# Four recurrent, attention and expert layers in one kernel: the instruction order is laid down on another timing model

## The chip, the core and the metric

The kernel runs on one core of a Trainium2 chip, as one program. The core has five engines with a queue each: TensorE for matmuls (PE in the profile, with its weight loads as PEld), VectorE (DVE), ScalarE (ACT), GpSimd (POOL) and SyncE (SP), which here only issues DMAs. The program gives each engine its instructions in a fixed order. The metric is the device time of one execution in microseconds (us), as the median of several runs.

## The reference

The input x holds 4 sequences of 1024 tokens with 128 features. Four layers follow one another; each has the form

```python
xn = _layernorm(x, axis=-1)
s = _Ln_attn_ref(xn, ...)          # the mixer
g = _silu(_Ln_ffn_ref(xn, ...))    # the gate
x = x + s * g
```

- Layer 0: a state space mixer (projection, rotation of the queries, RMS norm, a causal convolution of four taps, a recurrence over chunks, a gated norm) beside a feed-forward network whose activations and weights are rounded blockwise to a 4-bit float grid.
- Layer 1: attention between the 16 heads of one token, with entmax (a sort of 16 values, running sums, a threshold) in place of softmax, beside a mixture of eight experts, two of them chosen per token.
- Layer 2: a delta-rule recurrence with 2 x 16 states for each of 16 heads over the whole sequence, with a convolution, gates and a group norm, beside a second mixture of eight experts with bfloat16 products.
- Layer 3: causal attention over 1024 tokens with 16 heads of 8 features, with relative positions (the products of q with an embedding, shifted by one place per row), beside a feed-forward network.

## The kernel before

All arithmetic is on tiles of 128 partitions. x stays in SBUF (x_all) through layers 0 to 2 and goes through DRAM (x3) to layer 3. `tile_kernel` calls the layers one after the other.

Three things fix the order of the work.

First, the Python program. Its parts are generators that yield between small steps, and `weave` (L78) runs several of them side by side in proportion to their numbers of steps. In layer 0 a unit is half a sequence, eight units in all; `layer0` weaves the recurrence of a unit (`mixer0`), its feed-forward network (`ffn0`) and the first part of the next unit's mixer. Layer 1 does the same with `heads1` and `moe1`, and weaves in the preparation of layer 2's weights. In layer 3 the order is written out by hand: for each of 4 sequences and 4 groups of four heads, the eight query tiles of 128 rows are taken in the order 7, 0, 6, 1, 5, 2, 4, 3 (ORDER3), 128 units in all, and the loop in `layer3` issues in turn one step of the score stream (`scores3`), transposes of weights (L1807), a piece of the product with the values (`weigh3`), and work for later units.

Second, the scheduler of the Tile library. The program runs inside `with tile.TileContext(nc) as tc`. When this block ends, the library goes through all recorded instructions with their dependencies and lays down the order on each engine: it simulates the program, and an engine that is free in the simulation gets, of the instructions that are ready then, the one that came first in the program. Buffers of the tile pools are given out in the same pass. The order found so is fixed in the program that runs on the chip. Without an argument the simulation is the library's default one.

Third, the pools. The number of buffers of a pool limits how far work can run ahead. In layer 3 PSUM holds one tile of scores (four banks, tag sc), three of tag tr and one of tag o.

The lines that the rest speaks of:

- `Kit.fp4` (L166 on) rounds to the 4-bit grid in steps that alternate between DVE and POOL; its last product (L181, POOL) makes hm, which PE transposes at L567.
- `mixer0`: POOL rotates the queries into rq (L391, L392), ACT sums squares (L398, L399), DVE scales to hq (L403), PE transposes hq (L125, in the helper `transpose_tiles`). L486 is the matmul pg of a chunk's recurrence.
- `heads1`: POOL multiplies weights with values (L790, prod), DVE reduces the product (L785). L748 and L766 are POOL steps of entmax, L752 a running sum and L768 a comparison on DVE that need them.
- Layer 2: PE makes pv (L1185), DVE takes it out into V (L1186); POOL multiplies (L1395), DVE reduces into A (L1398); PE spreads expert shares (L224), DVE multiplies with them into xin (L1080).
- Layer 3: ACT copies the relative products from PSUM to r (L2035), SP stores them to DRAM (flat, L2038 and L2039) and loads them back sheared as rel (L2054 to L2060), POOL masks rel (L2064). PE makes scores (L2097), DVE takes them out of PSUM, adds rel and keeps a running minimum (L2105, L2112), ACT takes the exponential (L2119), DVE transposes the result in blocks of 32 (L1807, wT), PE multiplies with the values (L2133).

A score tile is read by DVE four times, once per head, and PE can fill it again only after that:

```python
sc = ps.tile([P, 4, 512], F32, tag="sc", name="score")
for j in range(4):
    nc.tensor.matmul(
        sc[:, j, 0 : last - first], q[at(j), 1 + t * P : 1 + n], kk[at(j), first:last], start=True, stop=True
    )
yield "products"
```

The function that the diff touches follows.

## Time and profile before

| | |
|---|---|
| median of three runs | 3198.6 us (3194.61 to 3202.84) |
| profiled execution, its own time | 3201.78 us |
| span of its instructions | 3199.8 us |
| mean granted TensorE clock | 0.738 of full |
| DVE busy | 2297.5 us (72%), 5558 instructions |
| PE busy | 2085.2 us (65%), 17041 matmuls |
| ACT busy | 1511.3 us (47%), 3278 instructions |
| POOL busy | 1165.9 us (36%), 1094 instructions |
| DMA | 333.13 MB, nearly all through one queue on SP |

How to read the lines that come later: a group or wait names the engine, what the instruction writes and the line of the kernel; "A <- B: total, times, longest" says that engine A stood idle in front of an instruction until B had ended, for so many microseconds in total. "issue" as a releaser means that the profile shows nothing that was waited for. A line of the timeline gives start, duration, engine, line, operation and operands, and in brackets the idle time of the engine in front of it with its releaser. In a table of stretches each row has its start and end, its length, the busy time of PE, PEld, DVE, ACT and POOL with their numbers of instructions, the granted clock of TensorE, the share of time in which the DMA engines moved data, and GB/s.

### The profile page before, as it was taken

How to read it: one execution, taken by the hardware profiler on the slowest of the kernel's cores; microseconds unless marked ns; L12 is line 12 of the kernel's file. 1: busy time of each engine (PE TensorE's matmuls, PEld its weight loads, DVE VectorE, ACT ScalarE, POOL GpSimd, SP SyncE). 2: the span in 40 equal slices, each digit the busy share in tenths (PEclk: the TensorE clock that was granted, in tenths of full speed). 3: DMA queues.
4: the chain of work that ended last, by engine and by line, in shares of the span. 5: the costliest groups of instructions: out<-in, count | busy, mean ns of one | idle time of the engine just before them, and what ended most of it. 6: DMA issues, size and time to landing. Idle time of an engine off the chain costs nothing. (4 is left out here: it accounts for less than half of the span.)

```text
span 3199.8 us, 47565 instructions
## 1 busy us (share of the span) xinstructions
PE 2085.2 (65%) x17041; PEld 1227.5 (38%) x17041; DVE 2297.5 (72%) x5558; ACT 1511.3 (47%) x3278; POOL 1165.9 (36%) x1094
## 2 busy tenths in 40 slices
PE   5787778577787766984443772455666666766754
PEld 2555556232233322661110232244444534544543
DVE  5555545878888886657777888567778787787777
ACT  3554544333333333435332562136766765764663
POOL 3334443134444444224468233232323322323322
PEclk9888888588878878995655575566766766766766
DMA  3000000100000000330343456248688677678772
GB/s 80 14 1 1 1 1 1 35 0 0 0 0 7 7 0 14 112 102 11 73 108 110 134 114 139 92 154 268 210 249 248 199 232 239 200 235 250 218 238 68
DMA packets 334064, 333.13 MB, mean 104 GB/s; under 512 B 25968, under 2 KB 307436, under 8 KB 328196
## 3 DMA queue, kind: packets, MB, share of 16 engines
q1 hardware_dynamic: 332676, 325.90, 34.4%
q10 hardware_dynamic: 1152, 4.19, 0.4%
q8 instruction: 134, 2.20, 0.3%
q14 instruction: 102, 0.84, 0.1%
HBM read 175.31 MB, written 154.14 MB: 103 GB/s over the span
## 5 line engine op out<-in xcount | busy, mean ns | idle before, releaser
L2119 ACT ACTIVATE neg<-neg,low 128x640 f32<-128x640 f32 (+7 forms) x512 | 390.1, 764 | 146.5 <-DVE low L2112 146.1
L1807 DVE STREAM_TRANSPOSE wT<-neg 128x640 f32<-128x640 f32 (+7 forms) x512 | 377.2, 761 | 18.0 <-ACT neg L2119 13.7
L2064 POOL TENSOR_SCALAR_AFFINE_SELECT rel<-rel 128x512 f32<-128x512 f32 x288 | 179.2, 635 | 549.5 <-DMA rel<-flat 388.2
L2112 DVE CUSTOM_DVE_ANT_0 neg<-score,rel,low 128x128 f32<-128x128 f32 (+3 forms) x448 | 211.8, 504 | 158.1 <-PE score L2097 62.8
L2133 PE MATMUL po<-wT,vb 128*32 128x64 f32 (+1 forms) x10240 | 258.5, 256 | 100.1 <-DVE wT L1807 52.2
L2133 PEld LDWEIGHTS po<-wT,vb 128*32 128x32 f32 x10240 | 211.4, 137 | 163.0 <-DVE wT L1807 76.9
L2097 PE MATMUL score<-k,q 32*128 32x512 f32 (+3 forms) x768 | 123.7, 557 | 180.6 <-DVE low L2112 180.0
L2035 ACT COPY r<-pr 128x512 f32<-128x512 f32 x256 | 135.2, 582 | 170.0 <-PE pr L2033 112.9
L2033 PE MATMUL pr<-emb,q 32*128 32x256 f32 x512 | 130.3, 445 | 70.8 <-ACT r L2035 52.6
L2112 DVE CUSTOM_DVE_ANT_0 neg<-score,rel 128x512 f32<-128x512 f32 (+3 forms) x320 | 149.6, 520 | 23.7 <-issue 9.6
L837 PE MATMUL pg<-xnT,w 128*128 128x512 f32 x256 | 149.3, 667 | 7.0 <-DVE h L841 3.9
L790 POOL TENSOR_TENSOR prod<-rest,kv 128x2048 f32<-128x2048 f32 x32 | 145.1, 4570 | 18.4 <-ACT rest L780 18.4
L840 ACT ACTIVATE h<-pg 128x512 f32<-128x512 f32 x128 | 75.9, 595 | 157.8 <-PE pg L837 154.4
L839 PE MATMUL pu<-xin,w 128*128 128x512 f32 x256 | 140.6, 632 | 12.9 <-DVE h L841 7.4
L828 PE MATMUL po<-h,w 128*128 128x512 f32 x256 | 129.7, 628 | 26.3 <-DVE h L841 26.3
L2097 PEld LDWEIGHTS score<-k,q 32*128 32x128 f32 x768 | 54.2, 232 | 223.8 <-DVE low L2112 177.8
L216 PE MATMUL pt<-ident,three 128*24 128x128 bf16 x64 | 9.2, 295 | 196.7 <-DVE three L213 196.7
L2033 PEld LDWEIGHTS pr<-emb,q 32*128 32x128 f32 x512 | 92.7, 270 | 111.9 <-ACT r L2035 72.6
L433 PE MATMUL px<-hT,xbcT 128*128 128x512 f32 x256 | 114.7, 592 | 0.0
L1086 PE MATMUL ph<-xin,upT 128*128 128x512 bf16 (+1 forms) x128 | 69.7, 575 | 65.7 <-DVE xin L1080 64.4
L1491 PE MATMUL read<-kt,const_sb 128*128 128x128 f32 x256 | 50.9, 371 | 90.3 <-POOL kt L1486 90.3
L785 DVE TENSOR_REDUCE s<-prod 128x128 f32<-128x2048 f32 x32 | 73.1, 2284 | 49.2 <-POOL prod L790 49.2
(633 smaller groups left out, 5749.5 us busy)
## 6 DMA issues: line engine op xcount, KB each, us to landing
flat<-r SPq DMA_DIRECT2D x128, 512.0 KB, 6.3
rel<-flat SPq DMA_DIRECT2D x112, 512.0 KB, 4.3
flat<-r SPq DMA_DIRECT2D x128, 256.0 KB, 6.3
rel<-flat SPq DMA_DIRECT2D x96, 256.0 KB, 4.7
kt<-kd SPq DMA_DIRECT2D x16, 512.0 KB, 4.6
qt<-qd SPq DMA_DIRECT2D x16, 512.0 KB, 5.7
kdc<-kdd SPq DMA_DIRECT2D x16, 512.0 KB, 8.6
ktc<-ktd SPq DMA_DIRECT2D x16, 512.0 KB, 6.2
```

The costliest lines, as they stand in the source:

```text
L790: nc.gpsimd.tensor_tensor(prod, attn.rearrange("p (t h g) -> p t h g", t=4, g=16)[:, t].unsqueeze(2).to_broadcast(each), kv[:, t, 1, :].re ...
L828: nc.tensor.matmul(po, W["w2"][:, e, c, :], h[:, c, :], start=(e == 0 and c == 0), stop=(e == 7 and c == 1))
L837: nc.tensor.matmul(pg, W["w1"][:, e, c * P : (c + 1) * P], xnT, start=True, stop=True)
L839: nc.tensor.matmul(pu, W["w3"][:, e, c * P : (c + 1) * P], xin, start=True, stop=True)
L1807: nc.vector.transpose(weights[at, pair][j][:, t % 2, 0 : (t + 1) * P], S[j][:, 0 : (t + 1) * P])
L2033: nc.tensor.matmul(to[:, m, :], q[at, t * P : (t + 1) * P], W["emb"][at, i, :], start=True, stop=True)
L2035: nc.scalar.copy(r[:, n], to)
L2064: nc.gpsimd.affine_select(out=rel[:, :, slot(back), :], in_=rel[:, :, slot(0), :], compare_op=op, fill=fill, base=0, pattern=[[0, 4], [-si ...
L2097: nc.tensor.matmul(sc[:, j, 0 : last - first], q[at(j), 1 + t * P : 1 + n], kk[at(j), first:last], start=True, stop=True)
L2112: nc.vector.tensor_tensor_reduce(out=neg[:, begin:last], in0=sc[:, j, begin - first : last - first], in1=rel[:, j, slot : slot + (last - b ...
L2119: nc.scalar.activation(neg[:, 0:n], neg[:, 0:n], AF.Exp, bias=here, scale=-1.0, accum_out=group["sums"][:, j, t : t + 1])
L2133: nc.tensor.matmul(o[32 * j : 32 * j + 32, 2 * pair + m.start : 2 * pair + 2, :], vb[:, kb % 4 * NT + kb // 4, j].rearrange("p a d -> p (a ...
```

## The change

The context is made with one more argument. With it the library's scheduler simulates on its timeline model in place of its default simulation, when it lays down the order of the instructions on each engine. The Python program, the tiles, the pools and the arithmetic are the same.

```diff
-    with tile.TileContext(nc) as tc:
+    with tile.TileContext(nc, schedule_with_timeline_sim=True) as tc:
         tile_kernel(tc, I, out)
```

## The prediction

> **What bounds the kernel now.** The change touches no instruction, only the order in which each engine gets its instructions. So I first read which engine limits each stage and how long it stands idle there; then who is waited for on that engine; then a few stretches of the timeline, to see whether such a wait is one that another order could fill. First, busy time by stretch (the stretches are cut at round times; layer 0 runs in the second one, layer 1 in the third, most of layer 2 in the fourth, the end of layer 2 and layer 3 in the fifth, where the first score matmul stands at 2152.8 us):
>
> ```profile
> core 0: us, PE busy (x) PEld busy (x) DVE busy (x) ACT busy (x) POOL busy (x), PEclk, DMA share, GB/s
> ...
> 60.00:560.00 500.00, 386.15 (x1858) 275.58 (x1856) 258.83 (x696) 256.33 (x590) 197.07 (x253) 0.87 0.02 7
> 560.00:1250.00 690.00, 501.99 (x1154) 206.57 (x1154) 556.87 (x787) 244.58 (x459) 264.41 (x116) 0.80 0.02 7
> 1250.00:1950.00 700.00, 422.24 (x1501) 198.76 (x1500) 514.94 (x1029) 297.78 (x587) 307.29 (x223) 0.69 0.34 95
> 1950.00:3150.00 1200.00, 728.06 (x11816) 516.94 (x11820) 905.04 (x2815) 683.15 (x1570) 368.90 (x457) 0.67 0.69 211
> ```
>
> PE limits layer 0 (386 of 500 us, 114 idle), DVE everything behind it (557 of 690, 515 of 700, 905 of 1200: 133, 185 and 295 idle). No stage has an engine that is always busy: 727 us of the 3090 are idle time of the limiting engine. That, and no more, is what an order can win; the busy sums stay. Second, who was waited for by that engine (us in total, times, longest), in layer 0, layer 1, layer 2 and layer 3:
>
> ```profile
> PE pt L125 <- DVE hq L403: 43.5, 7, 7.6
> PE pt L567 <- POOL hm L181: 42.2, 8, 5.7
> ```
> ```profile
> DVE s L785 <- POOL prod L790: 41.8, 24, 3.6
> DVE cum L768 <- POOL zz L766: 27.4, 8, 3.9
> DVE cum L752 <- POOL z L748: 11.9, 7, 2.1
> ```
> ```profile
> DVE V L1186 <- PE pv L1185: 44.3, 31, 6.7
> DVE A L1398 <- POOL gram L1395: 25.0, 17, 5.2
> DVE xin L1080 <- PE pb L224: 17.3, 25, 2.1
> ```
> ```profile
> DVE neg L2112 <- PE score L2097: 62.1, 17, 10.7
> DVE neg L2112 <- issue: 60.0, 30, 9.5
> DVE neg L2112 <- POOL rel L2064: 44.7, 14, 12.9
> ```
>
> The reader is to see two kinds. In layers 0 to 2 the waits are regular: seven or eight in the eight units of layer 0, 24 among the 32 products of layer 1. An order laid down by a simulation that takes a POOL or DVE step for shorter than it is would leave just that: the consumer is put at the head of its engine's queue too early, and everything behind it stands too. Sum: 43.5 + 42.2 = 85.7; 41.8 + 27.4 + 11.9 = 81.1; 44.3 + 25.0 + 17.3 = 86.6; together 253 us. In layer 3 they are rare and long: 17 waits for 192 score tiles (768 score matmuls, four to a tile), so 175 tiles are hidden already.
>
> Third, the timeline: one hole on PE in layer 0, and in layer 3 two score tiles whose wait DVE has nothing to hide with.
>
> ```profile
> 341.79 1.03 PE L510 MATMUL pst<-xdd,btm 128*128 128x256 f32 x4
> 348.77 1.11 PE L125 MATMUL pt<-const_sb,hq 128*128 128x128 f32 x4 [5.95 <-DVE hq L403]
> ...
> 352.45 0.63 PE L486 MATMUL pg<-xc 128*128 128x128 f32 x2
> ```
> ```profile
> 2422.64 0.75 DVE L2112 CUSTOM_DVE_ANT_0 neg<-score,rel,low 128x512 f32<-128x512 f32 x1 [0.68 <-PE score L2097]
> ...
> 2427.10 0.29 DVE L2112 CUSTOM_DVE_ANT_0 neg<-score,rel 128x128 f32<-128x128 f32 x1 [0.54 <-PE score L2097]
> ```
>
> PE stands 5.95 us in front of the transposes of hq. The pg matmul of L486 behind it (0.63 us) reads xc, which is older, and needed only to be ahead of it; what lies between them in the queue hangs on hq or on xq. So a good order fills a part of such a hole, not all of it.
>
> **The change, step by step.**
> *Instructions.* None is added, removed or resized by the program; 5558 on DVE, 17041 matmuls and 906 DMAs on SP stay. What can differ in number are semaphore waits and table loads on ACT. The trace has 177 ACT_TABLE_LOADs (the groups by line added up) of 1283 ns, 227 us. Between no load less (the functions needed stay) and half as many again (+114 us) I take nothing: ACT is busy at most 683 of 1200 us in any stretch and limits none. Without that cover, in layer 3, the exps (L2119) would be late for the transposes (L1807), which wait 13.7 us for them today.
> *How far the order moves.* Numbering the instructions as the program issues them and comparing with the order on each engine, the present order is displaced by a mean of 2.3 places on PE in layer 0, 5.2 on DVE in layer 1, 7.6 on DVE in layer 2 and 1.5 on DVE in layer 3 (there without L2112, whose numbers are not comparable). The generators fix the order by and large, and the scheduler moves things locally. I expect the new order to differ by as little, so the effect to be small.
> *Waits in layers 0 to 2.* Another order can remove between none and all of the 253 us, and can add waits as well. The nearest row is the hole above: 0.63 of 5.95 us could be filled by the one matmul that I could name, about a tenth; a lookahead over the other unit's work should find as much again. I take a fifth, **-51 us**. Next late there is the chain itself: POOL, ACT and DVE for hq and hm, under 55% busy, whose order cannot shorten it.
> *Layer 3, score tiles.* PE can fill the one score tile only when DVE has read it (L2097 waits 171 us for L2112 in this stretch, 102 times); DVE hides that behind transposes (L1807, 0.27 to 1.25 us each). Where none stands there, the wait is 0.54 to 0.68 us (above), 0.61 at the mean. At 175 covered tiles that is between 0 and +107 us; a better order could at most take the 62 away. This order is the one most nearly as the program gives it, so a new one has more to spoil than to mend: I take one tile in seven, 25 x 0.61 = **+15 us**.
> *Layer 3, SP and POOL.* All DMAs of the layer go through one queue on SP, where loads of rel wait 202.8 us for DVE and stores of r 193.5 us for ACT; a load put in front of a store holds it up. POOL waits 388 us for rel, but DVE only 44.7 for POOL. Between -45 and, if one load in ten of 208 comes later by a store's landing time (6.3 us), +131 I take 0: POOL's idle time covers it today.
> *Start and tail.* 60 us ahead and 50 behind; the last store waits for a chain that no order shortens: 0.
>
> The sum is -51 + 15 = -36 us. The profiled execution took 3201.8 us (span 3199.8); the median of the three runs is 3198.6, 3.2 less. I take the difference off the median: **3163 us**.
>
> [...] The rows say that the granted clock is 0.87 of full in layer 0 and 0.67 in layer 3. [...] The rows alone show the clock, not what it does in another order, and I leave it out.
>
> **Rivals.**
> *(a) No difference.* The new order comes out nearly as the old one, or the option does not act, or what is won in one stage is lost in the next: 3189 to 3208 us. For it: the small displacements, and that the limiting waits end on chains. Against it: three stages whose waits repeat in every unit.
> *(b) Slower: layer 3 loses its cover.* One mechanism: DVE's transposes no longer stand between the last read of a score tile and the first of the next. Price 0.61 us a tile, +107 us for all 175, and with no gain elsewhere 3306 us. It decides against the forecast's 51 us from 84 tiles on. For it: one score tile, DVE 75% busy and limiting, and a cover made of single transposes which ACT's exps release. Against: most tiles have two transposes ready there.
> *(c) Much faster.* Half of the 253 us goes and layer 3 keeps its order: -127, 3072 us. For it: the regularity of the waits. Against: the hole above.
>
> **Chances.** Faster by over 0.3%, which is about what a measurement of this kernel can tell from no change: 0.46 (the forecast and its neighbours 0.37, (c) 0.09). Within 0.3%: 0.12. Slower: 0.42, most of it (b) in part; the signs are nearly even because the same freedom that can fill a hole can open one. The range takes in (c) and nearly all of (b): 3075 to 3295 us; some 0.05 lies below and 0.1 above. The forecast's own range, one part in ten to one in three of the 253 with layer 3 at 0 to +30, is 3114 to 3203.
>
> **What would show it.** Right: PE's waits in front of L125 and L567 in layer 0, and DVE's in front of L785, shrink by a fifth or more; layer 3 takes as long as before, with about 40 waits of DVE for score tiles. Wrong: busy sums or the clock of a stage change by over 3%; more table loads with ACT limiting; or DVE waiting for score or rel far more often than 17 and 14 times. The forecast fails if these waits are chains rather than bad order, and if the new order moves far more than a few places.

## The result, and the profile after

| | before | after |
|---|---|---|
| median | 3196.8 us of 4 runs (3194.6 to 3202.8) | 3237.9 us of 4 runs (3233.0 to 3247.6) |
| ratio | | 1.0129 (95% interval 1.0101 to 1.0158) |
| profiled execution, span | 3201.8 us, 3199.8 us | 3247.6 us, 3245.9 us |
| DVE busy | 2297.5 us | 2408.5 us |
| ACT busy, instructions | 1511.3 us, 3278 | 1537.3 us, 3297 |

The change makes the kernel 1.3% slower (41 us by the medians); 36 us less were forecast. DVE, PE and POOL have as many instructions as before, ACT has 19 more. First to be read is where each layer begins and ends (first and last instruction of its lines in the trace; layer 1 without the two memsets at its head, L626 and L627; for layer 3 the stream of score matmuls, L2097):

| us | before | after | difference |
|---|---|---|---|
| start until layer 0's first instruction | 42.4 | 64.1 | +21.7 |
| layer 0 | 529.1 | 533.2 | +4.1 |
| layer 1 | 693.3 | 698.2 | +4.9 |
| layer 2 | 868.7 | 837.7 | -31.0 |
| layer 3, score stream | 1015.0 | 1060.3 | +45.3 |
| between and behind them | 51.3 | 52.4 | +1.1 |

The sum is the 46.1 us between the spans; it is 5 us more than between the medians, since the profiled execution of after is the longest of its four. Four things have to be explained, not one, and they have both signs. The table of stretches of after, cut at the layers, and below it that of before, cut at the same places of the program:

```profile
core 0: us, PE busy (x) PEld busy (x) DVE busy (x) ACT busy (x) POOL busy (x), PEclk, DMA share, GB/s
64.00:597.00 533.00, 405.20 (x1906) 293.14 (x1906) 279.34 (x713) 261.89 (x612) 201.87 (x260) 0.84 0.02 6
607.00:1304.00 697.00, 529.01 (x1154) 211.02 (x1153) 645.20 (x744) 242.43 (x454) 285.12 (x115) 0.80 0.02 5
1306.00:2144.00 838.00, 503.92 (x1848) 259.67 (x1848) 634.14 (x1341) 340.96 (x678) 365.10 (x265) 0.66 0.38 105
2154.00:3214.00 1060.00, 657.11 (x11752) 465.13 (x11748) 799.19 (x2537) 672.92 (x1513) 306.83 (x412) 0.67 0.70 216
```
```profile
42.00:571.00 529.00, 400.62 (x1911) 286.37 (x1910) 280.52 (x784) 267.80 (x622) 205.49 (x266) 0.87 0.02 7
580.00:1273.00 693.00, 511.08 (x1155) 207.81 (x1155) 559.64 (x750) 242.89 (x454) 274.37 (x115) 0.80 0.02 5
1275.00:2144.00 869.00, 498.72 (x1848) 261.37 (x1848) 634.33 (x1333) 342.78 (x680) 352.04 (x265) 0.67 0.36 101
2153.00:3168.00 1015.00, 644.90 (x11752) 454.92 (x11752) 786.68 (x2537) 642.87 (x1493) 307.52 (x412) 0.68 0.74 226
```

The reader is to see the second row: in layer 1 the busy time of DVE rises from 560 to 645 us with the same work, while the layer keeps its length. In layer 2 DVE's busy time is the same and the layer is 31 us shorter. In layer 3 ACT is 30 us busier, and DVE too is busier by 12.5 of the 45 us (799.2 against 786.7); the other 32.5 are idle time of DVE. The clock differs by 0.03 at most.

**Layer 1: waits became longer instructions.** The waits of after that answer to those of before, PE's in layer 0 (first two lines), then DVE's in layer 1 and in layer 2:

```profile
PE pt L125 <- DVE hq L403: 45.9, 8, 7.7
PE pt L567 <- POOL hm L181: 38.1, 9, 5.7
```
```profile
DVE s L785 <- POOL prod L790: 7.7, 5, 2.2
DVE cum L752 <- POOL z L748: 0.9, 1, 0.9
```
```profile
DVE V L1186 <- PE pv L1185: 31.0, 22, 5.8
```

In layer 0, cut at the layer, before had 50.1 and 48.2 us in the first two; in layer 2 it had 44.3. In layer 1, cut at the layer, it had

```profile
DVE s L785 <- POOL prod L790: 49.2, 28, 3.6
```

and 11.9 us at L752 and 27.4 at L768, which no longer stands in the list: 88.5 us have become 8.6. The forecast for that was a fifth; nine tenths went, and the layer gained nothing. Where they went is seen in the timeline, POOL's line first, then DVE's in the same time:

```profile
1139.81 9.31 POOL L790 TENSOR_TENSOR prod<-rest,kv 128x2048 f32<-128x2048 f32 x2 [3.04 <-ACT rest L780]
```
```profile
1139.30 0.66 DVE L698 TENSOR_TENSOR sorted<-sorted 128x384 f32<-128x384 f32 x1
1139.86 4.93 DVE L699 TENSOR_TENSOR sorted<-sorted 128x384 f32<-128x384 f32 x1
1144.70 0.68 DVE L841 TENSOR_TENSOR h<-h,pu 128x512 f32<-128x512 f32 x1
1145.30 4.38 DVE L698 TENSOR_TENSOR sorted<-sorted 128x512 f32<-128x512 f32 x1
```

A step of the sort (L698, L699: both operands in SBUF) takes 0.66 us just before POOL's product begins and 4.93 us beside it, about as long as one product (two in 9.31 us, so 4.65 at the mean); L841, one of whose operands lies in PSUM, takes 0.68 us in the same time (all 128 of it in after take 0.65 to 0.69 us; the 25 that lie wholly beside a POOL instruction 0.68 at the mean, the 71 beside none as well). In after, 62 of the 96 instructions of L698 have next to no POOL instruction beside them and take 0.50 us at the mean, the 10 that lie wholly beside one take 2.07, the 24 that lie partly beside one 2.10; in before 87 of 96 are alone (0.51 us; all shapes taken together). The 10 are a mixture: where a row of short sort steps is under way when a product begins, as at 718 us in after, they keep their 0.28 us, and the product takes 5.48 us, where the one at 1139.81 us takes 4.49. The order of before let DVE stand until POOL was done; that of after gives it the sort for this time, and the sort stands instead, as busy time. What holds the sort up beside POOL, and not L841, no run here shows.

**Start-up.** DVE's longest wait there in after, and ACT's:

```profile
DVE ln_rs L141 <- ACT ln_rs L140: 14.1, 1, 14.1
```
```profile
ACT bias L617 <- DMA bias<-in_L_attn_bq: 18.3, 1, 18.3
```

L617 scales the bias of layer 1, work for 580 us later. It depends on one transfer alone, and it stands near the front of ACT's queue, in before as well, where ACT waits 12.8 us for it. The transfer lands at 38 us in both; whatever stands behind it on ACT waits. In before DVE was well into the unpacking of layer 0's weights by then (its wait for ACT was 6.9 us); in after its queue has more of the layernorms first, so DVE waits for ACT and the weights wait behind that: PE takes the first of them (L316) at 53.1 us, in before at 24.7.

**Layer 3.** DVE's waits in after:

```profile
DVE wT L1807 <- ACT neg L2119: 56.7, 44, 5.3
DVE neg L2112 <- POOL rel L2064: 48.5, 7, 18.3
DVE neg L2112 <- PE score L2097: 47.9, 42, 4.7
DVE neg L2112 <- issue: 26.8, 13, 4.2
```

and the first and the third of them in before, in the same cut:

```profile
DVE wT L1807 <- ACT neg L2119: 13.7, 15, 5.0
DVE neg L2112 <- PE score L2097: 63.4, 18, 10.7
```

Those for scores are more and shorter, and less in sum; those for "issue" have halved (60.0 us in before). What has grown most is the first line: the transposes wait for exponentials. They also wait 21.3 us for PE's products with the values (L2133), against 4.2 in before. ACT's table loads in layer 3 (L1987, L1994 and L2119 together) have gone from 38 to 60, of 1.283 us each: 28.2 us. ACT's timeline in after, inside the first feed-forward network:

```profile
2280.26 1.28 ACT L1994 ACT_TABLE_LOAD   x1
2281.55 0.38 ACT L1994 ACTIVATE g<-po 128x256 f32<-128x256 f32 x1
2281.83 0.38 ACT L1987 ACTIVATE h<-pgu 128x256 f32<-128x256 f32 x1
2282.09 0.38 ACT L1988 COPY up<-pgu 128x256 f32<-128x256 f32 x1
2282.49 1.28 ACT L2119 ACT_TABLE_LOAD   x1
2283.79 0.61 ACT L2119 ACTIVATE neg<-neg,low 128x384 f32<-128x384 f32 x1
2284.31 0.19 ACT L2119 ACTIVATION_READ_ACCUMULATOR neg<-neg,low 128x1 f32 x1
2284.51 1.28 ACT L1987 ACT_TABLE_LOAD   x1
2285.81 0.38 ACT L1987 ACTIVATE h<-pgu 128x256 f32<-128x256 f32 x1
2286.09 0.37 ACT L1988 COPY up<-pgu 128x256 f32<-128x256 f32 x1
2286.47 1.28 ACT L2119 ACT_TABLE_LOAD   x1
```

From the first silu on: a load, one head's exponential, a load, the next silu, a load: three loads in 6 us. Of the sixteen stretches of 48 score matmuls, the second, sixth and fourteenth, which hold such a network, took 78.6, 77.5 and 75.2 us, against 65.7, 69.0 and 67.3 in before; the tenth, which holds one too, lost only 1.0. These three are 29 of the 45 us.

### The profile page after: what moved, and what is told of

Same layout as the page of the kernel before. It is cut to its first block, busy times and chain, and to the rows that moved or that the text cites. A ratio compares the mean times of both kernels' runs of the same rounds, so it can differ in the third digit from the quotient of the medians.

```text
span 3245.9 us, 47677 instructions
## 1 busy us (share of the span) xinstructions
PE 2125.1 (65%) x17041; PEld 1246.3 (38%) x17041; DVE 2408.5 (74%) x5558; ACT 1537.3 (47%) x3297; POOL 1191.5 (37%) x1094
## 5 line engine op out<-in xcount | busy, mean ns | idle before, releaser
L2119 ACT ACTIVATE neg<-neg,low 128x640 f32<-128x640 f32 (+7 forms) x512 | 391.2, 767 | 194.1 <-DVE low L2112 193.8
L1807 DVE STREAM_TRANSPOSE wT<-neg 128x640 f32<-128x640 f32 (+7 forms) x512 | 361.4, 753 | 78.7 <-ACT neg L2119 56.7
L2133 PE MATMUL po<-wT,vb 128*32 128x64 f32 (+1 forms) x10240 | 277.3, 267 | 72.6 <-DVE wT L1807 57.8
L2112 DVE CUSTOM_DVE_ANT_0 neg<-score,rel,low 128x128 f32<-128x128 f32 (+3 forms) x448 | 217.8, 518 | 95.0 <-PE score L2097 45.7
L2133 PEld LDWEIGHTS po<-wT,vb 128*32 128x32 f32 x10240 | 225.0, 145 | 142.0 <-DVE wT L1807 76.1
L2097 PE MATMUL score<-k,q 32*128 32x512 f32 (+3 forms) x768 | 125.7, 581 | 206.5 <-DVE low L2112 204.3
L2112 DVE CUSTOM_DVE_ANT_0 neg<-score,rel 128x512 f32<-128x512 f32 (+3 forms) x320 | 148.9, 520 | 64.9 <-POOL rel L2064 30.2
L828 PE MATMUL po<-h,w 128*128 128x512 f32 x256 | 145.0, 656 | 36.1 <-DVE h L841 36.1
L2097 PEld LDWEIGHTS score<-k,q 32*128 32x128 f32 x768 | 58.2, 245 | 245.9 <-DVE low L2112 171.6
L841 DVE TENSOR_TENSOR h<-h,pu 128x512 f32<-128x512 f32 x128 | 86.1, 676 | 18.1 <-ACT h L840 9.7
L2119 ACT ACTIVATION_READ_ACCUMULATOR neg<-neg,low 128x1 f32 x512 | 97.1, 190 | 0.0
L2105 DVE TENSOR_SCALAR_CACHE_REDUCE neg<-score 128x384 f32<-128x384 f32 (+2 forms) x192 | 79.3, 413 | 17.7 <-PE score L2097 17.7
## 6 DMA issues: line engine op xcount, KB each, us to landing
ktc<-ktd SPq DMA_DIRECT2D x16, 512.0 KB, 15.5
```

The source lines that it names most:

```text
L828: nc.tensor.matmul(po, W["w2"][:, e, c, :], h[:, c, :], start=(e == 0 and c == 0), stop=(e == 7 and c == 1))
L1807: nc.vector.transpose(weights[at, pair][j][:, t % 2, 0 : (t + 1) * P], S[j][:, 0 : (t + 1) * P])
L2097: nc.tensor.matmul(sc[:, j, 0 : last - first], q[at(j), 1 + t * P : 1 + n], kk[at(j), first:last], start=True, stop=True)
L2112: nc.vector.tensor_tensor_reduce(out=neg[:, begin:last], in0=sc[:, j, begin - first : last - first], in1=rel[:, j, slot : slot + (last - b ...
L2119: nc.scalar.activation(neg[:, 0:n], neg[:, 0:n], AF.Exp, bias=here, scale=-1.0, accum_out=group["sums"][:, j, t : t + 1])
L2133: nc.tensor.matmul(o[32 * j : 32 * j + 32, 2 * pair + m.start : 2 * pair + 2, :], vb[:, kb % 4 * NT + kb // 4, j].rearrange("p a d -> p (a ...
```

## The experiments

To keep orders apart from everything else, most kernels here fix the whole order: the program is recorded, and each instruction gets an edge, which sets the order only and needs no semaphore, from the one that is to stand in front of it on its engine.

```python
for one, two in zip(queue, queue[1:]):
    tc.add_manual_dep(traced[two], traced[one].name, mybir.DependencyInfo(
        mybir.DependencyClass.NoSync, mybir.DependencyReason.DATA), reason="order")
```

The queues come from building the program with and without the argument; `old[2]` are those of before, `new[2]` those of after. `mixed` takes the first set of queues and, for the stages n that the function at its end names (1 is layer 0, 4 is layer 3), the second; `old[3]` says which stage an instruction belongs to. The layers that keep the old order take as long in these kernels as in before (layer 2 takes 868.5 us in the fourth kernel below, 868.7 in before), so fixing an order costs nothing that these times show. The theory after reading the traces: the start loses by the held queue of ACT, layer 1 wins nothing since waits become contention, layer 2 wins by its order, layer 3 loses by its order, through the table loads. The rivals stand in the expectations.

### Which layers' orders cost and win

Four kernels. The first is after with one instruction moved (`later` puts the scale of L617 back by 40 places in ACT's queue):

```diff
+    order = mixed(new[2], old[2], old[3], lambda engine, n: False)
+    later(order, old[3], 40)
```

> The kernel after, each queue in the order of after, but one ScalarE instruction (the scale of layer 1's bias, L617) stands 40 places later in its queue. Theory: in after this instruction holds ScalarE for 18.3 us at the start, behind a transfer that lands at 38.4 us, and VectorE's layernorm behind it holds the unpacking of layer 0's weights; without it layer 0's first instruction comes at about 48 us instead of 64.1 and the whole takes some 16 to 20 us less than after: about 3220 us, 1.007 of before. Rival: VectorE's own order (layernorm ahead of the weights) is what makes the weights late; then layer 0 still begins after 60 us and the time stays near 3237 us (1.013).

Measured: 3225.6 us, 1.0088 (1.0071 to 1.0105). Layer 0 begins at 50.0 us instead of 64.1: the 14.1 us of DVE's wait, to the tenth. The theory's 16 to 20 were a little too much, and the rival has a part: 50.0 is still 7.6 us later than before's 42.4. For a fair comparison the instruction has to be out of the way on both sides, and the third of these kernels has it so in the old order: there layer 0 begins at 36.1 us. So 13.9 of the 21.7 us at the start come from the new order without this instruction, and 7.8 from its holding the new order longer than the old one (14.1 against 6.3). PE takes the first weight (L316) at 39.0 us here and at 24.9 there, and DVE's layernorms stand ahead of the weights; that they are the cause was not tried alone.

```diff
+    order = mixed(new[2], old[2], old[3], lambda engine, n: n == 4)
```

> The kernel after, with the instructions of layer 3 alone in the order that they have in the kernel before, on all five queues. Theory: the 45 us that layer 3 lost (score stream 1060 us against 1015) are its own order's: the stream takes about 1015 us again and the kernel about 3193 us (0.998 of before). Rival: they come with what layer 3 finds when it starts (a lower granted clock, transfers still under way), and not from its order: the stream stays near 1060 us and the kernel near 3237 us (1.013).

Measured: 3191.3 us, 0.9987 (0.9977 to 0.9998). The score stream takes 1009.4 us. The loss is the order's; what layer 3 finds at its start matters little.

```diff
+    order = mixed(old[2], new[2], old[3], lambda engine, n: n == 3)
+    later(order, old[3], 40)
```

> The kernel before, with the instructions of layer 2 alone in the order that they have in after, and the scale of L617 40 places later on ScalarE. Theory: layer 2 keeps the 31 us that it won in after (838 us against 869), and the start-up gives some 7 us (VectorE's wait for ln_rs was 6.9 us in before): about 3159 us, 0.988 of before. Rival: layer 2 won only because its input came in another order or later, or layer 3 pays the gain back: 3185 to 3200 us (0.996 to 1.001).

Measured: 3153.0 us, 0.9865 (0.985 to 0.9879). Layer 0 begins at 36.1 us (6.3 earlier than in before), layer 2 takes 829.3 us (39.4 less), layer 3 stays at 1012.1. **This kernel beats both.** In its layer 2 these are DVE's two longest waits:

```profile
DVE V L1186 <- PE pv L1185: 31.0, 22, 5.8
DVE xin L1080 <- PE pb L224: 19.8, 22, 2.0
```

DVE is busy for 632.0 us of 829 (634.3 of 869 in before): here the gain is idle time, with no instruction made longer. The 25.0 us at L1398 have left the head of the list and V's wait has shrunk by 13. Which moved instruction made each gain was not tried.

```diff
+    order = mixed(old[2], new[2], old[3], lambda engine, n: n == 4)
```

> The kernel before, with the instructions of layer 3 alone in the order that they have in after. Theory: it loses what layer 3 lost in after, 45 us: about 3242 us, 1.014 of before. Rival: the order of layer 3 costs nothing by itself: about 3197 us (1.000).

Measured: 3253.1 us, 1.0172 (1.0157 to 1.0187); the stream takes 1064.2 us, 49 more than in before. The order costs this wherever it is put. For the size of such differences: in the profiles of four kernels with layer 3 in the old order the stream takes 1008 to 1015 us (before is the longest), in three with the new order 1060 to 1066; layer 2 takes 865 to 869 us in the old order and 828 to 838 in the new one.

### One queue at a time in layer 3

The same as the last kernel, but only one engine is to take its new order. As two orders can contradict each other, the instructions are sorted by their places under all dependencies and buffer reuses, so other queues move where they must; the kernel holds the outcome as a table of steps from the program's order.

```diff
+    steps = np.frombuffer(zlib.decompress(base64.b85decode("".join(ORDER))), np.int16)
...
+    for n in np.arange(len(traced)) + steps:
```

By these tables the named queue comes to a mean of 0.3 (DVE), 0.8 (ACT), 1.3 (SP) and 2.5 places (PE) from after's order in layer 3, and no other queue moves by more than 1.3 from before's.

> The kernel before, with ScalarE's instructions of layer 3 alone in the order of after (other queues move only where a buffer or an operand forces it). Layer 3 then has after's 60 table loads instead of 38. Theory A (ScalarE's order is the cost): 22 loads of 1.283 us, 28 us, fall on the exponentials that the transposes wait for: layer 3 takes 20 to 50 us longer, about 3226 us, 1.009 of before or more, and most of it in the four stretches of 48 score tiles with the feed-forward in them. Theory B (VectorE's order) and theory C (SyncE's order): within 8 us of before (0.998 to 1.003).

> The kernel before, with VectorE's instructions of layer 3 alone in the order of after (transposes and layernorm statistics ahead of score reductions). Theory B (VectorE's order is the cost): its transposes stand at the head of the queue before their exponentials are done (in after VectorE waits 56.5 us there against 13.7 us in before), layer 3 takes 30 to 45 us longer, about 3232 us, 1.011. Theory A (ScalarE) and theory C (SyncE): within 8 us of before (0.998 to 1.003).

> The kernel before, with SyncE's transfers of layer 3 alone in the order of after. Theory C (SyncE's order is the cost): its loads of rel that wait for a buffer (321 us in after against 203 us) hold the stores and loads behind them, layer 3 takes 20 to 45 us longer, 1.006 to 1.014. Theories A and B: within 5 us of before (0.998 to 1.002).

> The kernel before, with TensorE's instructions of layer 3 in the order of after as far as buffers allow (mean displacement from before 6.9 places of the 9.0 in after); ScalarE's table loads in layer 3 rise from 38 to 46 with it. Theories A, B and C: no more than the 8 loads, 10 us, so 1.000 to 1.003. Rival D (TensorE's order, products of the feed-forward and the relative terms ahead of scores, is the cost): 20 to 45 us, 1.006 to 1.014.

Measured: ACT 1.0287 (1.0269 to 1.0305), DVE 1.0183 (1.0166 to 1.0200), SP 1.0262 (1.0241 to 1.0283), PE 1.0320 (1.0297 to 1.0343). DVE's alone costs as much as all five together (1.0172), each of the others more. Every theory had the queues that it didn't name within 0.3 or 0.4% of before, so none holds as it stood, and these runs settle nothing about the cause. They suggest something else: the queues of one plan belong together. In the kernel with SP's new order DVE waits for scores more than anything else, in that with PE's the score matmuls come late for the other reduction:

```profile
DVE neg L2112 <- PE score L2097: 96.2, 25, 18.1
```
```profile
DVE neg L2105 <- PE score L2097: 128.4, 41, 8.9
```

### The table loads taken out, and two other queues in program order

With whole plans again: layer 3 in the old and in the new order, without the need for most loads.

```diff
-                nc.scalar.activation(h[:, c, :], pgu[:, 0, :], AF.Silu)
+                nc.scalar.activation(h[:, c, :], pgu[:, 0, :], AF.Exp, scale=1e-3)
...
-            nc.scalar.activation(g[:, half, first : first + 2], po, AF.Silu)
+            nc.scalar.activation(g[:, half, first : first + 2], po, AF.Exp, scale=1e-3)
```

> The kernel before with all five queues of layer 3 in the order of after (as in the run before that measured 1.0172), and in layer 3's feed-forward the exponential of a thousandth of the operand in place of silu, so that ScalarE needs 4 table loads in layer 3 instead of 60 (the feed-forward's values are other ones; nothing else changes). Theory A (table loads on the exponentials' way are what layer 3 lost): its score stream falls from 1064 us to 1030 us or less, and stands at most 15 us above that of before with the same exponential. Theory E (the order loses by the places of its instructions, whatever the loads): the stream stays 35 to 50 us above that of before with the same exponential.

> The kernel before in its own order on every queue, with the same exponential in place of silu in layer 3's feed-forward: 4 table loads in layer 3 instead of 38. It is the bar for the run beside it. Theory A: 34 loads of 1.283 us are 44 us of ScalarE, mostly beside VectorE's work; the score stream falls from 1015 us to 995 to 1010 us (0.994 to 0.999 of before). Theory E: 1010 to 1015 us.

Measured: new order 3209.8 us, 1.0050 (1.0034 to 1.0066), stream 1022.3 us; old order 3188.8 us, 0.9978 (0.9969 to 0.9988), stream 1001.2 us. Without the loads the new order's stream gains 41.9 us and the old one's 13.8. The difference is 28 us; by the medians (43.3 us against 8.0) it is 35. The 22 additional loads take 28.2 us, so as nearly as these runs tell they cost at least their whole length. The four stretches with a feed-forward network go from 76.3, 78.9, 70.6 and 76.0 us to 65.6, 67.1, 63.5 and 67.4, against 65.0, 66.8, 66.4 and 66.8 of the old order without the loads: there nothing is left. The rows of the first of these stretches, with the loads and without:

```profile
2229.00:2306.00 77.00, 53.99 (x798) 38.51 (x798) 51.26 (x159) 55.91 (x118) 21.22 (x31) 0.68 0.51 160
```
```profile
2227.00:2293.00 66.00, 49.58 (x798) 35.42 (x798) 50.16 (x159) 40.06 (x103) 20.80 (x30) 0.77 0.57 178
```

ACT is 73% busy in the first, which looks like room; DVE, at the same work, stands 16 us without them and 26 with them. The gap between the two orders falls from 49 to 21 us (by the medians too, 21 remain). Theory A said at most 15, theory E at least 35, so neither holds as it stood: the loads are the larger part, and 21 us have another cause.

The next two leave the scheduler free on its timeline model and hold one queue of layer 3 to program order; both also hold the scale of L617.

```diff
+        at = len(nc.cur_bb.bb.instructions)
         layer3(k, W3, x3, out, eps5, ps, first)
+        in_order(tc, at, ENGINE)
```

Here ENGINE stands for `('Activation',)` in one kernel and `('DVE',)` in the other.

> The kernel after (the scheduler free on the other four queues and in the other layers), with ScalarE's instructions of layer 3 kept in program order, which leaves 20 table loads there instead of 60, and the scale of layer 1's bias kept in program order too. The second gives the 12 us of the run that moved it alone. Theory A: layer 3's score stream falls from 1060 us to 1015 us or less, the whole to about 3180 us (0.995 of before) or below. Theory E or B (the order of the other queues costs it): the stream stays at 1045 to 1066 us, the whole at 3210 to 3226 us (1.004 to 1.009).

> The kernel after with VectorE's instructions of layer 3 kept in program order (62 table loads in layer 3), the other queues left to the scheduler, and the scale of layer 1's bias kept in program order. Theory B (transposes put ahead of the score reductions are what layer 3 lost): the score stream falls from 1060 us to 1015 to 1025 us, the whole to about 3180 us (0.995). Theory A: the stream stays at 1050 us or more, the whole at 3215 us or more (1.006 and up).

Measured: ACT 3215.6 us, 1.0058 (1.0039 to 1.0076), stream 1046.1 us; DVE 3262.6 us, 1.0210 (1.0195 to 1.0226), stream 1095.9 us. The second gives theory B no support: with DVE's instructions where the program has them the layer is slower still. But its longest wait is one that neither order has in this size, transposes that wait 109.3 us for PE's products with the values (21.3 in after), so it does not rule the theory out. The first shows that few loads are no aim by themselves. It has 20, and 14 us less in the stream, but its stretches with a feed-forward network take 80 to 83.5 us. ACT now stands for the feed-forward's matmuls with exponentials queued behind it, and DVE stands for those:

```profile
ACT g L1994 <- PE po L1993: 76.1, 16, 10.5
```
```profile
DVE wT L1807 <- ACT neg L2119: 82.2, 31, 10.8
```

### The rest of layer 3, and layer 1 alone

In the new order of layer 3, the transposes on DVE are put later, where the old order has them on average; the other queues stay as they are (PE's moves by a mean of 0.1 places). The kernels hold the order as a table, as above. By it the transposes stand 3.5 places later, and not the 2.5 that the expectations name; their mean place is the old order's.

> Layers 0 to 2 as before, layer 3 in the order of after with the exponential in place of silu in its feed-forward (4 table loads), and on VectorE alone layer 3's transposes some 2.5 places later, so that they stand on average where before has them. Theory F (the rest of the loss, 21 us of score stream above before with the same exponential, is transposes that stand too near behind their exponentials: 40.6 us of waits against 7.2 us): these waits fall below 15 us and the stream goes from 1022 us to 1012 us or less (0.997 to 1.002 of before). Rival G (the rest is the sequence of the other queues, or the products that wait for the later transposes take the gain): the stream stays at 1018 us or more (1.003 to 1.010).

> The same with silu, so with after's 60 table loads in layer 3. Theory F: the score stream goes from 1064 us to 1050 us or less (1.013 of before or less), the table loads' 28 us staying. Rival G: 1060 us or more (1.016 and up).

Measured: 3212.9 us, 1.0050 (1.0031 to 1.0068), stream 1028.0 us without the loads; 3249.8 us, 1.0176 (1.0157 to 1.0194), stream 1059.3 us with them. The waits for exponentials do fall, but others rise, with no gain. After the new order without loads, the new order without loads and with later transposes:

```profile
DVE wT L1807 <- ACT neg L2119: 40.6, 39, 4.9
DVE neg L2105 <- PE score L2097: 18.6, 8, 8.4
```
```profile
DVE wT L1807 <- ACT neg L2119: 9.6, 7, 2.8
DVE neg L2105 <- PE score L2097: 41.1, 21, 7.1
```

Theory F falls. The wait was no cost by itself: taken away at one place it stood at the next.

```diff
+    order = mixed(old[2], new[2], old[3], lambda engine, n: n == 2)
```

> The kernel before with the instructions of layer 1 alone in the order of after. Theory H (VectorE's waits for GpSimd turn into longer VectorE instructions beside GpSimd): its waits at L785, L768 and L752 go from 88 us to about 10 us, its busy time in the stage rises by some 73 us, and the layer takes 693 to 700 us, so 0.999 to 1.003 of before. Rival (a fifth or more of those waits is time won, which after loses again through what layer 0 leaves behind): layer 1 takes 675 us or less, 0.994 or below.

Measured: 3206.6 us, 1.0028 (1.0014 to 1.0043). Layer 1 takes 698.9 us, 5.6 more than in before. DVE is busy for 647.0 of its 698 us (559.5 of 692), and one sort step and the reduction behind POOL's product read

```profile
L785 DVE TENSOR_REDUCE s<-prod 128x128 f32<-128x2048 f32 x32 | 72.8, 2275 | 7.7 <-POOL prod L790 7.7
L698 DVE TENSOR_TENSOR sorted<-sorted 128x512 f32<-128x512 f32 x24 | 40.8, 1701 | 0.4
```

against 49.2 us idle and 770 ns in before. Theory H holds: about 80 us less waiting, 87 us more busy time, and nothing won.

## Why the prediction was wrong

The forecast of -36 us and the 46 us of the two profiles lie 82 us apart: 29 in layers 0 to 2, 22 at the start, 30 in layer 3 and 1 between the layers. The signs of being wrong that the prediction names came up: the busy sum of DVE in layer 1 changed by more than 3% (560 to 645 us), and on DVE the order moved by more than a few places.

- **"The busy sums stay"** failed, and with it the -51 us. The waits that the prediction counts in layers 0 to 2 shrank by more than a fifth taken together: in layer 0 by 15%, in layer 1 by nine tenths, and the largest in layer 2 by 30%. But in layer 1 the new work in the hole contends with what DVE had waited for, and DVE's busy sum grew by 85 us. The three layers came to +4, +5 and -31, so -22 in place of -51. Layer 2 alone gave more than its share of a fifth of 86.6 us; as the moves that won it are not known, that the sign was right there is no proof of the mechanism.
- **"Start and tail: 0"** failed by +21.7 us. The step looked at chains and not at heads of queues: one ACT instruction that waits for a late transfer, as the row of L617 in before would have shown (12.8 us), costs 14.1 us in the new order and 6.3 in the old; the other 13.9 us are the new order's without it, with the weights of layer 0 unpacked later.
- **"I take nothing" for table loads** was the costliest step in layer 3. The bounds, none to +114 us, held the truth; the value did not. Its reason was ACT's share over a long stretch, 683 of 1200 us. The loads fall in four short stretches, on the exponentials that the transposes wait for: the cover that the text itself named, "the exps would be late for the transposes", was gone just there. It cost 28 us or more.
- **Score tiles, +15 us**: the count was right (42 waits; about 40 were forecast), the price was not. It was 0.61 us, from two rows, while the prediction's own 17 waits of 62.1 us are 3.7 us each; in after they are 1.1 us each and fell in sum. With the price and the sum wrong, the right count is luck. What layer 3 lost, 45 us, came by other ways. Rival (b), slower through lost cover, had the sign and the layer, and not the mechanism.
- **SP and POOL in layer 3: 0** held for POOL: DVE's wait for rel is 48.5 us (44.7). What SP's own order costs within the whole plan was not separated.
- **"By as little"** failed on DVE. By the queues of the two builds its instructions stand at a mean 15.5 places from where before has them in layer 1, 16.6 in layer 2 and 3.9 in layer 3; on PE in layer 0 it is 2.1. In layer 3 ACT's queue moved by a mean of 3.1 places, and that was enough for 22 loads: how far a queue moves tells little of what that costs.
- **The clock** stayed within 0.03 in every layer. Layer 0 went from 0.87 to 0.84, PE's busy time there rose by 4.6 us, and the layer lost 4.1; in each profile with this order in layer 0 the clock is 0.84 or 0.85. What made the clock lower was not tried.

Open: 21 us of layer 3, which are neither the loads nor the mean place of the transposes. They lie in the first, third, fourth and eleventh of its sixteen stretches (26 us more than in the old order, both without loads; the twelfth gives 6 back). The kernels with one queue changed cannot tell whose they are, since each lost more than that. The traces of the two kernels without loads narrow them down; layer 3 in the old order and in the new one:

```profile
2150.00:3152.00 1002.00, 638.06 (x11752) 448.95 (x11752) 784.79 (x2538) 597.96 (x1459) 307.71 (x412) 0.69 0.74 229
```
```profile
2152.00:3175.00 1023.00, 652.99 (x11754) 459.86 (x11754) 799.54 (x2538) 599.57 (x1457) 306.69 (x412) 0.67 0.73 224
```

15 of the 21 us are busy time of DVE. Its instructions are not longer (their durations add up to 1.3 us less); they overlap less. L2112 needs the minimum that L2105 finds. In the old order a transpose mostly stands between the two and starts before L2105's reading of the minimum has ended; in the new order L2112 mostly follows at once and starts 0.04 us after it (old order, then new):

```profile
2178.70 0.08 DVE L2105 DVE_READ_ACCUMULATOR neg<-score 128x1 f32 x1
2178.70 1.24 DVE L1807 STREAM_TRANSPOSE wT<-neg 128x1024 f32<-128x1024 f32 x1
```
```profile
2189.02 0.08 DVE L2105 DVE_READ_ACCUMULATOR neg<-score 128x1 f32 x1
2189.14 0.48 DVE L2112 CUSTOM_DVE_ANT_0 neg<-score,rel,low 128x256 f32<-128x256 f32 x1
```

L2112 follows at once 156 times of 192 instead of 13; at 0.12 us each the 143 are 17 us. That these make up most of the 21 us is possible and not shown. No kernel changed this alone; in the one without loads and with later transposes L2112 follows at once 114 times and DVE's busy time in the stream is 9 us shorter, but its idle time is 14 us longer. And PE too is 15 us busier in the new order, at a clock of 0.67 against 0.69. Also open is which moves won layer 2's 31 to 39 us.

## What to carry to other kernels

Another model in a scheduler gives another plan, not a better one in each stage: time the stages apart, and take the order of each from where it was shorter (here 0.9865 of before, from one stage of the slower kernel and one instruction moved). Before a wait is counted as winnable, ask what would run in its place and whether that can run beside the work waited for. Look at the heads of the queues at the start, and count table loads in the stretches where two functions meet, not over the layer.

## What the runs showed of the hardware

- A sort step on DVE (L699 in after, both operands in SBUF) that starts 0.05 us behind a POOL tensor_tensor took about as long as that: 4.93 us beside a product of 4.65 us (two in 9.31), 0.66 us for its like ahead of it. Where a row of sort steps was under way first (718 us in after), they kept their 0.28 us and the product took 5.48 us instead of 4.49. L841, with an operand in PSUM, took 0.65 to 0.69 us beside POOL and without it.
- 22 table loads of 1.283 us, 28.2 us in all, in a layer where ACT is 63% busy, cost 28 us by the profiles and 35 by the medians.
- On DVE, L2112 directly behind L2105, whose result it needs, starts 0.04 us after its end (median of 156 in after); a transpose (L1807) in its place starts 0.08 us before that end (median of 164 in before).
- In layer 3 four queues, changed singly towards the order of a plan that costs 1.7% as a whole, cost 1.8 to 3.2% each.
